# Ranks of two edge tiles from one ScalarE sum, and one set of node rows for both feature halves, in the first layer of a graph network

## The chip, the cores and the metric

The kernel runs on one core of a Trainium2 chip: TensorE (PE in the profile, with its weight loads as PEld), VectorE (DVE), ScalarE (ACT), GpSimd (POOL) and the DMA queues, of which SyncE's (SP) carries most direct transfers. The metric is the device time of one execution in microseconds (us), as the median of repeated executions. Lower is better.

## The reference, cut to what matters

Two graph layers with residual connections and layer norms, on 12,500 nodes with 256 features and 200,000 edges sorted by `dst`.

```python
# first layer: row = src, col = dst
feat = relu(einsum('nd,ohdk->ohnk', x, W) + b)        # o = 2 halves (self, neighbour), 4 heads of 32
feat_self, feat_nei = feat
att_s = leaky(feat_self . a_self); att_n = leaky(feat_nei . a_neigh)
edge_w = (att_s[:, row] + att_n[:, col]) * adj_vals
agg = segment_sum(edge_w * feat_nei[:, col], row)     # sum over the edges of each src node
# both halves: centred and scaled per head, put side by side, then
x = layernorm(x + first_layer)
# second layer: messages relu([x[src], x[dst]] @ W_msg + b), summed by dst, update, layernorm
```

The edges come sorted by `dst`, but the first layer sums by `src`. So the kernel sorts the messages by block of `src`.

## The kernel before, in words

**Three stages run one after the other.** The first builds a log: for each group of 14 tiles of 128 edges (1,792 edges, 112 groups), it makes the messages and scatters them into a DRAM table (`log`), sorted by the block of 128 nodes that their `src` lies in (98 blocks). The second stage reads the log block by block, sums it with matmuls, and finishes the first layer. The third does the second layer with gathers. The change lies in the first stage, and in the loads that the second makes of what the first wrote.

**One group in the first stage, its sort half** (`sort_tasks`). `widen` (L564, ACT) copies the block numbers of the first 7 tiles out to 7 x 99 columns; `hot` (L568, DVE) compares them with a table to make one-hot rows `A`; `hot_b` (L572, DVE) does the other 7 tiles straight from the block numbers with a broadcast operand. `pair` (L576) adds tile t and tile t+7. `ranks`, `quarter`, `rows`, `begins` count and place on PE, ACT and DVE; `keep_v` (L606, ACT) brings the place table `V` (128 x 100) to SBUF. `place_mm` (L622, L624, PE) puts `V` plus 4096 times the one-hot rows into PSUM, in chunks of 5, 5 and 4 tiles, in two buffers `wp`. `place_pick` (L651, ACT) then reads one tile at a time: a relu with bias -4096 leaves the one wanted entry of each row, and `accum_out` sums the row. Each pick is two records in the profile: ACTIVATE and ACTIVATION_READ_ACCUMULATOR. There are 14 picks a group. `split` (L658, L659, L660, DVE) turns the 14 ranks into a partition `q` and a slot `r`; `hot_r` (L664), `hot_q` (L674) and `goods` (L669, DVE) turn them into one-hot operands, and `permute` (L681, PE) carries the edges' data to their places. `extras` (L697, L698, DVE) puts source and weight into the message tile `m`. Destinations go through DRAM (`rel_out` L701, `rel_in` L705, on SP's queue) and come back as a wide row for `hot_n` (L709, DVE). `message` (L718, PE) and `evict` (L725, ACT) make the messages, and four `scatter`s (L731, POOL) write them. `index` (L644, DVE) computes the row indices that the scatters use.

**Its feature half** (`feat_tasks`). A group needs neighbour features of a window of 128 rows that starts at a register's value, `xw`. The self features are made 128 rows at a time in block order, from rows of their own, `xb`, in groups 0 to 97 (98 blocks). Both are loaded on SP's queue (`load_group`, L432, L438), transposed on PE (L457, L460), kept by ACT (`keep`, L466), projected by four 128-column matmuls and a bias matmul (L471, L474), and go through `relu` (L482, ACT) and, on DVE, `att_mult` (L486), `mean_sum` (L491), `att_sum` (L495), `centre` (L500), `leaky_n` (L506) and `leaky_s` (L525). In groups 98 to 111 there are no `xb` rows, and these instructions are half as wide. `out_f` (L528, SP) writes the centred self half to the DRAM table `selfd`; its attention terms stay in SBUF, in `atts`.

**What sets the order.** PE, ACT, DVE and SP execute in the order in which the program emits them. That order is a table: `AT[name]` is a task's place, a group is 256 places after the one before (`TG`), and all tasks of all groups are sorted by `256 * group + AT[name]` and emitted. So a task named 100 of group 3 follows one named 300 of group 2. The numbers set the order alone; an engine starts each instruction as soon as the earlier ones on it and the semaphores allow. Every eighth group also has the `m_` tasks, which prepare the edge data of the next eight groups.

**The second stage** loads `x` and `selfd` per span of up to four blocks (`load_y`), multiplies the summed log by `atts` (`heads_a`, L986) and scales the self half (`own_s`, `own_c`, `own_d`).

Of the kernel before, what the change touches and what calls it, by code (L numbers as in the profile page):

```python
# [11 lines left out]
def _warn_once_fixed(msg, *args, **kwargs):  # L12
# [28 lines left out]
    "widen": -453, "hot": -365, "hot_b": -265, "pair": -179, "ranks": -86, "quarter": -64, "rows": -29,  # L41
    "begins": 13, "keep_begins": 55, "keep_v": 51, "shift": 161, "reach": 262, "steps": 227, "steps_keep": 243,
    "steps_low": 256, "target": 313, "index": 400, "place_mm0": 52, "place_mm1": 63, "place_mm2": 204,
    "pick0": 73, "pick1": 78, "pick2": 78, "pick3": 87, "pick4": 123, "pick5": 144, "pick6": 156, "pick7": 170,
    "pick8": 179, "pick9": 219, "pick10": 229, "pick11": 239, "pick12": 249, "pick13": 280, "split": 339,
    "hot_r": 358, "goods": 374, "hot_q": 371, "permute": 424, "rel_keep": 435, "extras": 477, "rel_turn": 502,
    "rel_row": 552, "rel_out": 574, "rel_in": 595, "hot_n": 959, "message0": 997, "evict0": 1053,
    "message1": 1032, "evict1": 1063, "message2": 1056, "evict2": 1082, "message3": 1065, "evict3": 1121,
    "message4": 1101, "evict4": 1165, "message5": 1188, "evict5": 1203, "scatter0": 1120, "scatter1": 1146,
    "scatter2": 1197, "scatter3": 1206, "load": -331, "transposes": 47, "keep": 68, "project": 80, "relu": 295,  # L50
    "att_mult": 355, "mean_sum": 459, "att_sum": 438, "centre": 467, "leaky_n": 498, "part0": 584, "part1": 636,
    "part2": 665, "part3": 705, "leaky_s": 585, "out_f": 634, "m_load": -1689, "m_cast0": -1234,
    "m_cast1": -1433, "m_col0": -1201, "m_keep0": -1125, "m_col1": -698, "m_keep1": -614, "m_col2": -941,
    "m_keep2": -861, "m_block": -1073, "m_place": -877, "m_high": -378, "m_rest": -285, "m_mid": 263,
    "m_low": 351, "m_win": -76, "m_turn": -866, "m_pairs": -710, "m_mask": -535, "m_count": 210,
}
BIG = 4096.0
# [43 lines left out]
def kernel(  # L101
# [45 lines left out]
    selfd = dram.tile([ROWS, HD], FT, name="selfd")  # L147
# [12 lines left out]
    atts = consts.tile([P, NB, H], FT, name="atts")  # L160
# [55 lines left out]
    with ExitStack() as l0:  # L216
# [28 lines left out]
        nc.vector.memset(nbig, -BIG)  # L245
        quart = dcp.tile([P, 1], FT, name="quart")
# [178 lines left out]
        xb = {}  # L425
        F3 = {}

        def load_group(g):
            if g < NG:
                b = base_reg(g) if g else 0  # L430
                xw[g] = xin.tile([P, D], FT, name="xw")
                nc.sync.dma_start(xw[g], x[bass.ds(b, P), :])  # L432
            if g < NB:
                xb[g] = xin.tile([P, D], FT, name="xb")
                n = min(P, N - g * P)
                if n < P:
                    nc.vector.memset(xb[g], 0.0)
                nc.sync.dma_start(xb[g][:n], x[g * P:g * P + n, :])  # L438

        def feat_tasks(g):  # L440

            ww, bb = g < NG, g < NB
            o0, o1 = (0 if bb else 1), (2 if ww else 1)
            lo, hi = o0 * HD, o1 * HD
            st = {}

            def flat(t):
                return t[:, lo:hi]

            def heads(t):  # L450
                return t[:, lo:hi].rearrange("p (a k) -> p a k", k=32)

            def transposes():
                tp = ps.tile([P, 512], FT, name="tp", bufs=1)
                if ww:
                    for c in range(2):
                        nc.tensor.transpose(tp[:, c * P:(c + 1) * P], xw[g][:, c * P:(c + 1) * P], ident)  # L457
                if bb:
                    for c in range(2):
                        nc.tensor.transpose(tp[:, (2 + c) * P:(3 + c) * P], xb[g][:, c * P:(c + 1) * P], ident)  # L460
                st["tp"] = tp

            def keep():
                xT = feat.tile([P, 4, P], FT, name="xT")
                a, z = (0 if ww else 2), (4 if bb else 2)
                nc.scalar.copy(xT[:, a:z].rearrange("p c q -> p (c q)"), st["tp"][:, a * P:z * P])  # L466
                st["xT"] = xT

            def project():
                fp = bank[g][:, 0:D] if ww else ps.tile([P, 512], FT, name="fs")[:, 0:D]  # L470
                nc.tensor.matmul(fp[:, lo:hi], ones3, bias3[:, lo:hi], start=True, stop=False)  # L471
                for o in range(o0, o1):
                    for c in range(2):
                        nc.tensor.matmul(  # L474
                            fp[:, o * HD:(o + 1) * HD], st["xT"][:, (2 + c) if o == 0 else c, :],
                            w0s[:, c, o * 4:(o + 1) * 4, :].rearrange("p a k -> p (a k)"),
                            start=False, stop=(o == o1 - 1 and c == 1))
                st["fp"] = fp

            def relu():  # L480
                st["R"] = feat.tile([P, D], FT, name="R")
                nc.scalar.activation(flat(st["R"]), st["fp"][:, lo:hi], AF.Relu)  # L482

            def att_mult():
                st["tm"] = feat.tile([P, D], FT, name="tm")
                nc.vector.tensor_tensor(flat(st["tm"]), flat(st["R"]),  # L486
                                        atb.rearrange("p o h k -> p (o h k)")[:, lo:hi], op=OP.mult)

            def mean_sum():
                st["m"] = feat.tile([P, 2 * H], FT, name="m")  # L490
                nc.vector.tensor_reduce(st["m"][:, o0 * H:o1 * H], heads(st["R"]), AX.X, OP.add)  # L491

            def att_sum():
                st["a"] = feat.tile([P, 2 * H], FT, name="a")
                nc.vector.tensor_reduce(st["a"][:, o0 * H:o1 * H], heads(st["tm"]), AX.X, OP.add)  # L495

            def centre():
                st["F"] = feat.tile([P, D + H], FT, name="F", bufs=4)
                m = st["m"][:, o0 * H:o1 * H]
                nc.vector.scalar_tensor_tensor(  # L500
                    heads(st["F"]), m[:, :, None].to_broadcast([P, (o1 - o0) * H, 32]), -1.0 / 32, heads(st["R"]),
                    op0=OP.mult, op1=OP.add)

            def leaky_n():
                a = st["a"][:, H:2 * H]
                nc.vector.scalar_tensor_tensor(st["F"][:, D:D + H], a, 0.2, a, op0=OP.mult, op1=OP.max)  # L506


            def part(k):
                def f():  # L510
                    n = st["F"][:, HD:]
# [11 lines left out]
            def leaky_s():  # L523
                a = st["a"][:, 0:H]
                nc.vector.scalar_tensor_tensor(atts[:, g, :], a, 0.2, a, op0=OP.mult, op1=OP.max)  # L525

            def out_f():
                nc.sync.dma_start(selfd[g * P:(g + 1) * P, :], st["F"][:, 0:HD])  # L528

            w = lambda f: f if ww else None  # L530
            k = lambda f: f if bb else None
            return dict(transposes=transposes, keep=keep, project=project, relu=relu,
                        att_mult=att_mult, mean_sum=mean_sum, att_sum=att_sum, centre=centre, leaky_n=w(leaky_n),
                        part0=w(part(0)), part1=w(part(1)), part2=w(part(2)), part3=w(part(3)),
                        leaky_s=k(leaky_s), out_f=k(out_f))
# [12 lines left out]
        def sort_tasks(g):  # L548
# [5 lines left out]
            CH = [(0, 5), (5, 5), (10, 4)]  # L554
# [7 lines left out]
            def widen():  # L562
                st["bx"] = srt.tile([P, h, NBX], BF, name="bx")
                nc.scalar.copy(st["bx"], blk[c][:, j * GT:j * GT + h, None].to_broadcast([P, h, NBX]))  # L564

            def hot():
                st["A"] = srt.tile([P, GT, NBX], BF, name="A", bufs=3)
                nc.vector.tensor_tensor(st["A"][:, :h], iotab[:, :h], st["bx"], op=OP.is_equal)  # L568

            def hot_b():  # L570
                b = blk[c][:, j * GT + h:j * GT + GT, None].to_broadcast([P, h, NBX])
                nc.vector.tensor_tensor(st["A"][:, h:], iotab[:, h:], b, op=OP.is_equal)  # L572
# [32 lines left out]
            def keep_v():  # L605
                nc.scalar.copy(small("v", NBE, FR, p=P), st["V"])  # L606
# [10 lines left out]
            def place_mm(i):  # L617
                def f():
# [3 lines left out]
                    nc.tensor.matmul(o, identr, st["v"][:, None, :].to_broadcast([P, n, NBE]),  # L622
# [23 lines left out]
            def place_pick(t):  # L646
                def f():
                    i, k = divmod(t, 5)
                    if t == 0:
                        small("sl", GT, p=P)  # L650
                    nc.scalar.activation(small("junk", NBX, BF, p=P), st["w", i][:, k * NBE:k * NBE + NBX], AF.Relu,  # L651
                                         bias=nbig, accum_out=st["sl"][:, t:t + 1])
                return f

            def split():
# [1035 lines left out]
```

## Time and profile before

| What | Value |
|---|---|
| median of 10 runs | 4409.63 us (4402.7 to 4414.29) |
| the profiled execution | 4414.53 us, its span 4412.8 us |
| busy over the span | PE 3698.7, PEld 3132.3, DVE 3159.6, ACT 2372.6, POOL 2660.0 us |
| first stage | the first `hot_q` (L674) starts at 29.4 us, the last at 1052.9 us, the last message matmul (L718) at 1075.3 us |
| second stage | its log matmuls (L972) from 1087.9 to 1998.1 us |
| L651, the picks | 1,568 ACTIVATE, 604.8 us busy, and 1,568 accumulator reads, 477.4 us busy |

A row of groups reads: line, engine, operation, output <- inputs, shapes, count, then busy time and the mean ns of one instruction, then the idle time of the engine just before them and what ended it. A mean is the length of the record. Records of one engine overlap, so what an instruction costs its engine when it is full is the distance from its start to the next start, which the timeline shows. A windows row gives, for a stretch of the span, the busy time of each engine with its instruction count, the granted TensorE clock, and the DMA share.

### The profile page before, as it was taken

To read this page: it belongs to the slowest core of one execution; us is meant where nothing else is said; L and a number is where in the kernel's file an instruction comes from. 1 tells how busy PE (TensorE), PEld (TensorE's weight loads), DVE (VectorE), ACT (ScalarE), POOL (GpSimd) and SP (SyncE) were. 2 spreads that over 40 slices of the span, in tenths; PEclk is the share of its full clock that TensorE was granted. 3 is DMA by queue.
4 is the path that set the end of the run, shared out by engine and by line. 5 is a ranking of instruction groups with operands and counts; after the bars stand their busy time and mean duration, and the time that the engine had idled before them with its cause. 6 is when DMAs were issued, how large, how long until landed. Compare 5 with 4: busy or idle time off the path is not lost. (4 is left out here: it accounts for less than half of the span.)

```text
span 4412.8 us, 82564 instructions
## 1 busy us (share of the span) xinstructions
PE 3698.7 (84%) x24976; PEld 3132.3 (71%) x24976; DVE 3159.6 (72%) x9205; ACT 2372.6 (54%) x8379; POOL 2660.0 (60%) x2542
## 2 busy tenths in 40 slices
PE   8999999997999999996777777777777777777776
PEld 6888888876888888885666666666566666656665
DVE  9999999997999999995555555555555555555555
ACT  7999999996222222224444444444444444444444
POOL 2545555555666666665666666666666666666664
PEclk9999999998999999998888888888898888888888
DMA  5877766666666666664555555555555555545553
GB/s 187 277 266 273 247 216 216 218 202 215 181 192 191 191 191 191 191 183 132 143 143 143 141 141 146 140 142 144 141 143 143 143 143 142 146 138 143 143 143 109
DMA packets 470159, 763.55 MB, mean 173 GB/s; under 512 B 76202, under 2 KB 313504, under 8 KB 469712
## 3 DMA queue, kind: packets, MB, share of 16 engines
q1 hardware_dynamic: 339552, 415.13, 33.0%
q0 software_dynamic: 110848, 327.87, 24.3%
q10 hardware_dynamic: 19312, 15.21, 1.1%
q8 instruction: 204, 3.34, 0.3%
q14 instruction: 243, 1.99, 0.2%
HBM read 559.81 MB, written 198.12 MB: 172 GB/s over the span
## 5 line engine op out<-in xcount | busy, mean ns | idle before, releaser
L1346 POOL DMA_INDIRECT gb<-pd,srcf x1563 | 1501.0, 960 | 889.0 <-issue 492.5
L1424 PE MATMUL agg<-gb,o 128*128 128x256 f32 x3126 | 941.6, 429 | 346.9 <-ACT gb L1407 234.1
L1405 DVE TENSOR_TENSOR gb<-qp,gb 128x512 f32<-128x512 f32 x781 | 531.4, 680 | 757.0 <-remote 368.3
L1424 PEld LDWEIGHTS agg<-gb,o 128*128 128x128 f32 x3126 | 647.6, 215 | 520.4 <-ACT gb L1407 282.9
L731 POOL DMA_INDIRECT log<-m,ix x448 | 545.6, 1218 | 531.7 <-ACT rT L693 195.5
L1407 ACT ACTIVATE gb<-gb 128x512 f32<-128x512 f32 x781 | 487.4, 627 | 675.8 <-DVE gb L1405 483.9
L972 PE MATMUL sum<-lg,o 128*128 128x256 f32 x3724 | 838.3, 379 | 12.9 <-DVE o L964 12.8
L972 PEld LDWEIGHTS sum<-lg,o 128*128 128x128 f32 x3724 | 696.0, 189 | 112.5 <-POOL lg L959 12.4
L964 DVE TENSOR_SCALAR o<-iotap,lg 128x128 f32<-128x128 f32 x1862 | 613.2, 397 | 42.9 <-PE sum L972 35.1
L651 ACT ACTIVATE junk<-wp,nbig 128x99 bf16<-128x99 f32 x1568 | 604.8, 461 | 1.4 <-PE wp L624 1.0
L1383 PE MATMUL qp<-qh,oT 128*128 128x256 f32 x1563 | 595.4, 400 | 2.8 <-issue 1.9
L959 POOL TENSOR_TENSOR lg<-lg 128x512 f32<-128x512 f32 x392 | 429.6, 1108 | 229.6 <-DMA lg<-log 169.9
L651 ACT ACTIVATION_READ_ACCUMULATOR junk<-wp,nbig 128x1 f32 x1568 | 477.4, 318 | 0.0
L1383 PE MATMUL qp<-ql,oT 128*128 128x256 f32 x1563 | 438.1, 300 | 0.3 <-issue 0.3
L718 PE MATMUL mp<-F,oT 128*128 128x132 bf16 x5376 | 419.3, 222 | 20.0 <-ACT m L725 8.3
L718 PEld LDWEIGHTS <-oT 128*128 128x128 bf16 x5376 | 344.0, 99 | 52.3 <-issue 18.9
L1391 ACT ACTIVATE o<-iotac,rel 128x128 f32<-128x128 f32 x782 | 267.9, 391 | 177.5 <-PE agg L1424 49.8
L725 ACT COPY m<-mp 128x396 f32<-128x396 f32 (+1 forms) x672 | 352.3, 569 | 15.1 <-PE mp L718 10.0
L1383 PEld LDWEIGHTS qp<-qh,oT 128*128 128x128 f32 x1563 | 330.6, 212 | 29.3 <-PE agg L1424 2.3
L1383 PEld LDWEIGHTS qp<-ql,oT 128*128 128x128 f32 x1563 | 329.3, 211 | 24.8
L1387 DVE TENSOR_TENSOR o<-iotac,rel 128x256 f32<-128x256 f32 x390 | 161.5, 414 | 247.4 <-PE agg L1424 68.0
L890 PE MATMUL qm<-wms,xT 128*128 128x256 f32 x224 | 96.7, 521 | 254.4 <-ACT xT L885 211.6
(263 smaller groups left out, 6561.8 us busy)
## 6 DMA issues: line engine op xcount, KB each, us to landing
lg<-log SPq DMA_DIRECT2D x392, 268.0 KB
dr<-in_dst_dram SPq DMA_DIRECT2D x781, 128.0 KB
rr<-reld SPq DMA_DIRECT2D x112, 512.0 KB
log<-zero SPq DMA_DIRECT2D x101, 268.0 KB
gb<-pd,srcf POOLq DMA_INDIRECT x1563
lg<-log SPq DMA_DIRECT2D x98, 201.0 KB
xw<-in_x_dram SPq DMA_DIRECT2D x112, 128.0 KB
xw<-x1d SPq DMA_DIRECT2D x112, 128.0 KB
```

Source lines behind the costliest of these rows:

```text
L651: nc.scalar.activation(small("junk", NBX, BF, p=P), st["w", i][:, k * NBE:k * NBE + NBX], AF.Relu, bias=nbig, accum_out=st["sl"][:, t:t + 1])
L718: nc.tensor.matmul(mp[:, r * (HD + H):(r + 1) * (HD + H)], st["oT"][:, r0 + r], F3[g][:, k], start=(k == 0), stop=(k == 2))
L725: nc.scalar.copy(st["m"][:, r0:r0 + n, 0:HD + H], st.pop(("mp", i))[:, :n * (HD + H)].rearrange("p (r w) -> p r w", r=n))
L731: ins = nc.gpsimd.indirect_dma_start(out=log[:, :], out_offset=bass.IndirectOffsetOnAxis(ap=st["ix"][:, k:k + 1], axis=0), in_=st["m"][:, ...
L959: e.tensor_tensor(t[:, 1, :n, 0:HD].rearrange("p r (h k) -> p r h k", h=H), t[:, 0, :n, 0:HD].rearrange("p r (h k) -> p r h k", h=H), t[:, ...
L964: nc.vector.tensor_scalar(o[:, r], iotap, t[:, 0, r, MW - 2:MW - 1], t[:, 0, r, MW - 1:MW], op0=OP.is_equal, op1=OP.mult)
L972: nc.tensor.matmul(sums[b], o[:, r], t[:, :, r, 0:HD], start=(k == 0 and r == 0), stop=(k == NK - 1 and r == n - 1))
L1346: nc.gpsimd.indirect_dma_start(out=gb[s][:r, i], out_offset=None, in_=pd[:, :], in_offset=bass.IndirectOffsetOnAxis(ap=srci[:r, t:t + 1], ...
L1383: nc.tensor.matmul(qp[:r, i], oT[:, i * P:i * P + r], q, start=(k == 0), stop=(k == 1))
L1405: nc.vector.tensor_tensor(z, qp, z, op=OP.add)
L1407: nc.scalar.activation(z, z, AF.Relu)
L1424: nc.tensor.matmul(agg[g], o[:r, i], z[:r, i], start=(j == 0 and i == 0), stop=lastmm)
```

## The change: packed picks, a full widen, one set of rows, and a new order

Six edits and a new table of places:

1. The place table is kept twice, once as it is and once times 2048 (`keep_w`, a new ACT instruction). `place_mm` adds the plain one to even tiles and the other to odd tiles, in chunks of 4, 4, 4 and 2 tiles; the one-hot factor is 2^23 in place of 4096. One `place_pick` now reads two tiles (2 x 99 columns) and sums both into one number, even rank plus 2048 times odd rank: 7 picks a group.
2. The numbers are taken apart again by `unpack` (one ACT instruction on 128 x 7) and two more DVE instructions on 128 x 7 at the head of `split`.
3. `widen` copies all 14 tiles, and `hot_b` reads the copy as `hot` does.
4. The self half is projected from the window rows `xw` too. The `xb` rows, their loads, transposes and copies go; two matmuls of 256 columns take the place of four of 128. All 112 groups now make both halves, and `out_f` writes 132 columns (self half and its attention terms) to a window of `selfd` that starts at the register's value. Windows overlap, and write the same values where they do.
5. `atts` goes; the second stage loads 132 columns per row, and `heads_a` reads the attention terms there (the tile `fs` has three buffers for two).
6. The copy of the source column into `m` leaves `extras` (DVE) and becomes `src_keep` (ACT).

```diff
 AT = {
-    "widen": -453, "hot": -365, "hot_b": -265, "pair": -179, "ranks": -86, "quarter": -64, "rows": -29,
...
-    "pick8": 179, "pick9": 219, "pick10": 229, "pick11": 239, "pick12": 249, "pick13": 280, "split": 339,
...
+    "widen": -324, "hot": -281, "hot_b": -274, "pair": -190, "ranks": -115, "quarter": -70, "rows": -56,
+    "begins": -10, "keep_begins": 37, "keep_v": 33, "shift": 133, "reach": 236, "steps": 165, "steps_keep": 227,
+    "steps_low": 283, "target": 292, "index": 365, "keep_w": 37, "place_mm0": 64, "place_mm1": 77,
+    "place_mm2": 216, "place_mm3": 244, "pick0": 103, "pick1": 108, "pick2": 164, "pick3": 179, "pick4": 247,
+    "pick5": 247, "pick6": 250, "unpack": 267, "split": 308, "hot_r": 370, "goods": 402, "hot_q": 360,
+    "permute": 453, "rel_keep": 457, "extras": 491, "src_keep": 520, "rel_turn": 513, "rel_row": 535,
...
-BIG = 4096.0
+BIG = 2.0 ** 23
+PACK = 2048.0
...
         def load_group(g):
...
-            if g < NB:
-                xb[g] = xin.tile([P, D], FT, name="xb")
...
+            xreg[g] = base_reg(g) if g else 0
+            xw[g] = xin.tile([P, D], FT, name="xw")
+            nc.sync.dma_start(xw[g], x[bass.ds(xreg[g], P), :])
...
             def project():
...
+                nc.tensor.matmul(fp, ones3, bias3, start=True, stop=False)
+                for c in range(2):
+                    nc.tensor.matmul(fp, st["xT"][:, c, :], w0s[:, c].rearrange("p a k -> p (a k)"),
+                                     start=False, stop=(c == 1))
...
+            def leaky_s():
+                a = st["a"][:, 0:H]
+                nc.vector.scalar_tensor_tensor(st["F"][:, 0:H], a, 0.2, a, op0=OP.mult, op1=OP.max)
...
             def out_f():
-                nc.sync.dma_start(selfd[g * P:(g + 1) * P, :], st["F"][:, 0:HD])
+                nc.sync.dma_start(selfd[bass.ds(xreg[g], P), :], st["F"][:, 0:H + HD])
...
-            CH = [(0, 5), (5, 5), (10, 4)]
+            CH = [(a, min(4, GT - a)) for a in range(0, GT, 4)]
...
             def widen():
-                st["bx"] = srt.tile([P, h, NBX], BF, name="bx")
-                nc.scalar.copy(st["bx"], blk[c][:, j * GT:j * GT + h, None].to_broadcast([P, h, NBX]))
+                st["bx"] = srt.tile([P, GT, NBX], BF, name="bx")
+                nc.scalar.copy(st["bx"], blk[c][:, tl, None].to_broadcast([P, GT, NBX]))
...
             def hot_b():
-                b = blk[c][:, j * GT + h:j * GT + GT, None].to_broadcast([P, h, NBX])
-                nc.vector.tensor_tensor(st["A"][:, h:], iotab[:, h:], b, op=OP.is_equal)
+                nc.vector.tensor_tensor(st["A"][:, h:], iotab[:, h:], st["bx"][:, h:], op=OP.is_equal)
...
+            def keep_w():
+                nc.scalar.activation(st["v"][:, NBE:], st["V"], AF.Copy, scale=PACK)
...
-            def place_pick(t):
+            def place_pick(k):
                 def f():
-                    i, k = divmod(t, 5)
...
-                    nc.scalar.activation(small("junk", NBX, BF, p=P), st["w", i][:, k * NBE:k * NBE + NBX], AF.Relu,
-                                         bias=nbig, accum_out=st["sl"][:, t:t + 1])
+                    i, t = k // 2, 2 * k % 4
...
+                    nc.scalar.activation(
+                        small("junk", 2 * NBX, BF, p=P).rearrange("p (t b) -> p t b", b=NBX),
+                        st["w", i][:, t * NBE:(t + 2) * NBE].rearrange("p (t b) -> p t b", b=NBE)[:, :, :NBX],
+                        AF.Relu, bias=nbig, accum_out=st["s7"][:, k:k + 1])
...
+            def unpack():
+                nc.scalar.activation(small("t7", h, p=P), st["s7"], AF.Identity, bias=nhalf, scale=1.0 / PACK)
+
             def split():
-                sl = st["sl"]
+                sl = small("sl", GT, p=P)
+                odd = sl.rearrange("p (k w) -> p k w", w=2)[:, :, 1]
+                nc.vector.tensor_scalar(odd, st["t7"], MAGIC, -MAGIC, op0=OP.add, op1=OP.add)
+                nc.vector.scalar_tensor_tensor(sl.rearrange("p (k w) -> p k w", w=2)[:, :, 0], odd, -PACK, st["s7"],
+                                               op0=OP.mult, op1=OP.add)
...
             def extras():
                 m = st["m"] = msgp.tile([P, NR, MW], FT, name="m")
-                nc.vector.tensor_copy(m[:, :, MW - 2], st["go"][:, :, 1])
                 nc.vector.tensor_reduce(m[:, :, MW - 1], st["go"][:, :, 2:5], AX.X, OP.add)
+
+            def src_keep():
+                nc.scalar.copy(st["m"][:, :, MW - 2], st["go"][:, :, 1])
...
-                                    atts[:, b:b + n, :, None].to_broadcast([P, n, H, 32]), op=OP.mult)
+                                    fs.pop(q)[:, :n, 0:H, None].to_broadcast([P, n, H, 32]), op=OP.mult)
```

## The prediction on record

> **What bounds the kernel now.** I read the page's busy slices first, to see which stage the change lies in, then the windows of that stage, then the waits of each engine in it, and last the groups by shape and the timeline of one group.
>
> ```profile
> DVE  9999999997999999995555555555555555555555
> ACT  7999999996222222224444444444444444444444
> ```
>
> One slice is 110 us. In the first nine (the stage that builds the log) ACT and DVE are both full. From the tenth, ACT falls to 2: the second stage isn't ACT's. So an edit that relieves ACT can pay in the first stage alone, and there only if DVE lets it. The windows (us, then busy time and count per engine, clock, DMA share) show the same:
>
> ```profile
> 200.00:400.00 200.00, 190.56 (x2345) 161.28 (x2344) 193.54 (x605) 196.03 (x979) 101.33 (x85) 1.00 0.79 269
> 400.00:620.00 220.00, 211.65 (x2611) 179.41 (x2609) 213.49 (x666) 216.26 (x1072) 116.95 (x95) 1.00 0.71 241
> 620.00:920.00 300.00, 291.32 (x3611) 247.59 (x3610) 294.87 (x930) 299.53 (x1493) 164.00 (x132) 1.00 0.66 217
> 990.00:1050.00 60.00, 56.90 (x728) 48.16 (x728) 55.75 (x180) 60.00 (x317) 30.15 (x28) 1.00 0.61 200
> ```
>
> From 620 to 920 us ACT is busy 299.5 of 300 us, DVE 294.9, PE 291.3 (columns: PE, PEld, DVE, ACT, POOL). In this stretch the answer on DVE's waits is empty, and so is ACT's. DVE's missing 5 us are gaps of 0.03 us between an instruction and one that reads its result. So **DVE has no spare time either**: two engines are full at once, at 9.16 us a group (`hot_q` starts at 626.8 us and, 24 groups on, at 846.7). In 200 to 1000 us DVE waited on others for 6 us in all:
>
> ```profile
> DVE ix L644 <- DMA log<-m,ix: 2.2, 2, 1.5
> DVE ix L644 <- PE mp L718: 1.1, 1, 1.1
> ```
>
> **The change part by part.** A full engine's price is the distance from start to start, so I take prices from one group's timeline and use the shape rows to see that they repeat.
>
> *ACT.* Picks start at 700.35, 700.68 and 701.00: 0.325 us each, 14 make 4.55. A copy costs 0.48 for 512 columns (699.67 to 700.15) and 0.15 for 132 (703.87 to 704.02), so 0.87 ns a column; 99 more columns add 0.09. Seven picks of 198: 7 x 0.415 = 2.9, saving 1.65. `xT` of 256 columns costs 0.27 (as `relu`, 706.98 to 707.25) for 0.48: -0.21 in 98 groups. Added: 693 columns of `widen` +0.60, `keep_w` +0.13 (as `keep_v`, 707.40 to 707.53), `unpack` +0.14 (as `quarter`, 704.41 to 704.55), `src_keep` +0.06 (as `rel_keep`, 704.02 to 704.08). Sum: -0.93 us a group; in the last 14, where `relu` doubles (+0.10) and `xT` saves nothing, -0.62. Over the stage: 98 x 0.93 + 14 x 0.62 = 100 us less ACT work. That is the size of the edit, not its worth, since DVE stays.
>
> *DVE.* These lines are the price list (line, shape, count, then busy us and mean ns; below, the timeline: start, length):
>
> ```profile
> L572 DVE TENSOR_TENSOR A<-iotab,blk 128x693 bf16<-128x693 bf16 x33 | 28.8, 873 | 0.0
> ...
> L568 DVE TENSOR_TENSOR A<-iotab,bx 128x693 bf16<-128x693 bf16 x32 | 16.4, 511 | 0.0
> ```
>
> ```profile
> 713.17 0.41 DVE L491 TENSOR_REDUCE m<-R 128x8 f32<-128x256 f32 x1
> 713.61 0.43 DVE L500 SCALAR_TENSOR_TENSOR F<-m,R 128x256 f32<-128x256 f32 x1
> 713.96 0.18 DVE L697 COPY m<-mp 128x16 f32<-128x16 f32 x1
> 714.04 0.20 DVE L698 TENSOR_REDUCE m<-mp 128x16 f32<-128x48 f32 x1
> ...
> 716.18 0.17 DVE L658 SCALAR_TENSOR_TENSOR sl<-sl,twin 128x14 f32<-128x14 f32 x1
> 716.38 0.18 DVE L659 TENSOR_SCALAR q<-sl 128x14 bf16<-128x14 f32 x1
> 716.60 0.17 DVE L660 TENSOR_TENSOR r<-sl,q 128x14 bf16<-128x14 f32 x1
> 716.69 0.42 DVE L486 TENSOR_TENSOR tm<-R,atb 128x256 f32<-128x256 f32 x1
> ```
>
> - `hot_b` takes the form of `hot`: 873 to 511 ns, -0.36.
> - The copy L697 leaves: 713.96 to 714.04, -0.08.
> - `centre` (L500) reads what L491 wrote just before it, and starts 0.44 after it; the same reduce L495, with an unrelated successor, is followed after 0.33 (711.97 to 712.30). In the new order `mean_sum` and `centre` are apart: -0.11.
> - `split` grows from three dependent instructions to five. Each that the next one waits for costs 0.20 to 0.22 (L658, L659); the last costs 0.09. Two more: +0.42.
>
> Sum: **-0.13 us a group**. DVE's relief from `hot_b` is nearly eaten by the unpacking. The dependent pair is not in the trace on 7 columns; between 14 and 7 nothing should change, as the time is start-up. Bounds: from 0.08 each (an independent small one, L697) to 0.22, so the sum lies between -0.39 and -0.11. I take 0.21, the row of the same chain.
>
> In the last 14 groups DVE also gains width: L486, L491, L495 and L500 were 298, 278, 278 and 296 ns and become 430, 410, 410 and 424 (+0.52), and `leaky_s` adds 0.07. There ACT is the full engine (60.0 of 60) and DVE has 55.75, which is 8.09 us of each 8.7 us group. With +0.59 - 0.13 DVE reaches 8.55, and its gaps of 0.15 make 8.7. So those groups stay where they are: 0.
>
> [...]
>
> *PE.* The two `xb` transposes go (-0.14, 607.14 to 607.28); four projections of 128 columns become two of 256, the same columns; the `place_mm` columns are the same in one more pair, whose fixed part I put at 0.09 from the 500- and 400-column pairs (0.54 and 0.45 start to start). Net -0.05, off the path as long as DVE is fuller.
>
> *SP and DMA.* 98 loads of 128 KB go. `out_f` issues 14 more and waits for the write before it, a group ago: nothing, as SP has nine microseconds for five issues. `rel_in` and `load` are named later, but SP waits only for `rT` and for the `rel_out` landing, so in fact it issues them early in the slot. In the second stage PE is 200 of 200 us busy (1200 to 1800 us): wider `fs` rows cost nothing there. *POOL*: four scatters a group as before, half busy.
>
> *Fill and drain*: 29 us before the first `hot_q` and 22 us after the last are chains of latency through the same engines; I leave them, within 2 us.
>
> Sum: 98 x -0.13 = -13, last 14 groups 0, on the profiled execution's 4414.5 us (span 4412.8 and 1.7 around it): 4401.5. The median of the runs is 4.9 below that execution, so **4396.5 us**, -0.3%.
>
> **The rivals.**
>
> *A. ACT was the limit and all its relief shows:* 4409.6 - 100 = 4310. For it: ACT's 299.5 of 300. Against: DVE's waits are empty over 300 us; an engine that never waits cannot be sped up by another.
>
> *B. PE takes over.* PE's 291.3 of 300 is 8.90 us a group, DVE's new need 9.03. Light groups (8.62 us, without `m_` tasks) would ask 8.5 of DVE, below PE's average, and PE cannot catch up fully in the heavy ones (10.2 us) with two buffers. If half the groups give nothing, 49 x 0.13 = 6 us remain: 4403, within what a run can tell. Against: matmul records are pipelined, and PE's weight loads, which run beside them, fill 247.6 of 300. PE also has 4.7 us of waits on `rows` there, so it isn't full.
>
> *C. Slower: DVE waits in `split`.* The first new instruction reads `unpack`, which stands on ACT behind three picks in a row (1.25 us), `src_keep` and `relu` (0.33), all behind `permute` and two `place_mm` on PE. Behind `goods`, DVE has some 3.8 us of other work until `split`; the chain over PE (0.95) and ACT (0.06 + 0.04 + 0.27 + 1.25 + 0.06 + 0.14) needs 2.8, and a little for hand-overs. So 0.9 us of slack, if PE is on time. If PE comes late by more, DVE stands still, every group, and everything queued behind `split` with it (`pair`, `hot_q`, `index`, `goods`, on which PE's `permute` waits). Each 0.1 us is 11 us; the gain is gone from 0.13 us a group on, and at 0.3 us: 4409.6 + 112 x 0.17 = 4429.
>
> *D. `hot_b` stays at its old price* though it reads `bx` (its half starts 693 columns in, at an odd element). Then -0.36 falls away: +0.23 x 112 = 4435. Against: `pair` (L576) reads that same odd half of `A` in 515 ns; an output at an odd element beside dense inputs is in no row. [...]
>
> **How the numbers follow.** Forecast 0.52, A 0.03, B 0.22, C 0.19, D 0.04. The forecast's own range runs from the cheap end of the pair (98 x 0.39 = 38: 4371) to the dear one (4399). The range takes most of it, B and C's middle, and leaves out A, D and C's tail: 4375 to 4426. A difference of 0.2% (8.8 us) is about what runs of this kernel tell from none. Faster than that: 0.53. Within: 0.25, B and some ends of its neighbours. Slower: 0.22, C and D.
>
> **What would show it.** In 620 to 920 us of the changed kernel: DVE near 295 with no waits and 24 groups in 217 us; ACT down to about 270 with idle time; `hot_b`'s row at about 511 ns; starts of the new pair 0.2 us apart. If DVE's waits name `unpack` it is C; if they name PE's matmuls, B. I am wrong if the small instructions cost much less than 0.2 us, or if `index`, whose place moves from 218 to 166 places behind the scatter that frees its buffer, begins to wait for that landing in many groups: its 2.2 us of waits would grow.

## The result: slower, 4444.32 us

| | before | after |
|---|---|---|
| median of the runs | 4408.15 us (4402.7 to 4414.29, 28 runs) | 4444.32 us (4433.74 to 4449.16, 8 runs) |
| ratio | | 1.008, 95% interval 1.0071 to 1.0088 |
| profiled execution, span | 4414.53, 4412.8 us | 4434.49, 4432.7 us |
| last message matmul of the first stage starts at | 1075.4 us | 1102.5 us |
| log matmuls of the second stage, first to last | 911 us | 911 us |

The change costs 36 us, where a gain of 13 was forecast. In the two profiled executions the first stage is 27 us longer, the second is the same, and the third came out 7 us shorter; so in this pair the loss lies in the first stage. The profiled execution of the changed kernel is at the low end of its runs, which spread over 15 us, so the pair differs by 20 us where the medians differ by 36; what makes the runs spread is not settled.

The busy slices of the changed kernel: in the first nine, neither ACT nor DVE is full any more.

```profile
DVE  8999999997899999995555555555555555555555
ACT  7898989997122222223444444444444444444444
```

The windows of the first stage (us, then busy time and count of PE, PEld, DVE, ACT, POOL, clock, DMA share):

```profile
200.00:400.00 200.00, 186.90 (x2194) 158.15 (x2190) 186.50 (x604) 177.15 (x716) 115.50 (x84) 0.98 0.73 245
400.00:620.00 220.00, 206.25 (x2478) 175.56 (x2479) 208.46 (x681) 198.82 (x809) 127.76 (x93) 1.00 0.68 227
620.00:920.00 300.00, 283.35 (x3389) 241.29 (x3387) 286.06 (x934) 273.85 (x1102) 178.68 (x127) 0.99 0.59 198
990.00:1050.00 60.00, 56.39 (x673) 47.88 (x672) 57.13 (x189) 53.95 (x218) 38.17 (x27) 1.00 0.61 198
```

From 620 to 920 us PE, DVE and ACT are all less busy (291.3 to 283.4, 294.9 to 286.1, 299.5 to 273.9); POOL alone is busier (164.0 to 178.7), and still idle for two fifths of the time. When the engines that were full no longer are, and the stage is longer, they wait for each other. The largest of DVE's waits, 200 to 1000 us (who, for whom, us in all, times, longest):

```profile
DVE rows L565 <- ACT rows L561: 8.9, 23, 1.9
DVE ix L622 <- DMA log<-m,ix: 3.4, 6, 1.1
DVE mi L362 <- ACT srcf L352: 1.9, 6, 0.4
DVE ix L622 <- issue: 1.8, 4, 0.8
DVE ix L622 <- PE mp L707: 1.4, 2, 1.2
DVE rows L565 <- issue: 0.9, 4, 0.3
DVE ix L622 <- PE wp L602: 0.9, 2, 0.5
```

There are two places: `rows` (DVE) stands for `quarter` (ACT), and `index` for the landing of the scatters whose buffer it takes. The names in the second are not to be trusted singly: the waits of that one line, 9.0 us in all, bear six names in the view. The same view for PE:

```profile
PE mp L707 <- ACT m L687: 18.0, 41, 1.2
PE mp L668 <- DVE mv L656: 6.1, 23, 0.4
PE fs L569 <- DVE rows L565: 5.5, 7, 0.8
```

PE's largest wait is for `src_keep` (L687), the copy moved to ACT. The DVE instructions themselves are as forecast. The first two lines are groups by shape (busy us, mean ns), the rest is the timeline of one group:

```profile
L543 DVE TENSOR_TENSOR A<-iotab,bx 128x693 bf16<-128x693 bf16 x32 | 16.5, 517 | 0.2
L546 DVE TENSOR_TENSOR A<-iotab,bx 128x693 bf16<-128x693 bf16 x32 | 16.4, 512 | 0.0
```

```profile
715.55 0.16 DVE L641 TENSOR_SCALAR sl<-t 128x7 f32<-128x7 f32 x1
715.75 0.17 DVE L642 SCALAR_TENSOR_TENSOR sl<-sl,s 128x7 f32<-128x7 f32 x1
715.95 0.18 DVE L645 SCALAR_TENSOR_TENSOR sl<-sl,twin 128x14 f32<-128x14 f32 x1
```

`hot_b` fell from 873 to 512 ns, and the new pair starts 0.20 us apart.

### The profile page after: what moved, and what is told of

The parts are those of the page before. It is cut to its first block, busy times and chain, and to the rows that moved or that the text cites. A ratio compares the mean times of both kernels' runs of the same rounds, so it can differ in the third digit from the quotient of the medians.

```text
span 4432.7 us, 81040 instructions
## 1 busy us (share of the span) xinstructions
PE 3697.6 (83%) x24612; PEld 3129.1 (71%) x24612; DVE 3162.6 (71%) x9332; ACT 2309.8 (52%) x7147; POOL 2738.0 (62%) x2542
## 5 line engine op out<-in xcount | busy, mean ns | idle before, releaser
L720 POOL DMA_INDIRECT log<-m,ix x448 | 620.4, 1385 | 483.8 <-ACT v L583 304.5
L962 PE MATMUL sum<-lg,o 128*128 128x256 f32 x3724 | 838.6, 379 | 12.4 <-POOL lg L949 11.4
L629 ACT ACTIVATE junk<-wp,nbig 128x198 bf16<-128x198 f32 x784 | 331.0, 439 | 28.5 <-PE fs L558 18.7
L714 ACT COPY m<-mp 128x396 f32<-128x396 f32 (+1 forms) x672 | 295.8, 442 | 68.7 <-PE fs L558 35.0
L1367 DVE TENSOR_SCALAR oT<-dr,baseP 128x256 fp32r<-128x256 int32 x782 | 282.2, 361 | 11.2 <-DMA dr<-in_dst_dram 11.2
```

Source lines behind the costliest of these rows:

```text
L629: nc.scalar.activation(small("junk", 2 * NBX, BF, p=P).rearrange("p (t b) -> p t b", b=NBX), st["w", i][:, t * NBE:(t + 2) * NBE].rearrang ...
L714: nc.scalar.copy(st["m"][:, r0:r0 + n, 0:HD + H], st.pop(("mp", i))[:, :n * (HD + H)].rearrange("p (r w) -> p r w", r=n))
L720: ins = nc.gpsimd.indirect_dma_start(out=log[:, :], out_offset=bass.IndirectOffsetOnAxis(ap=st["ix"][:, k:k + 1], axis=0), in_=st["m"][:, ...
L962: nc.tensor.matmul(sums[b], o[:, r], t[:, :, r, 0:HD], start=(k == 0 and r == 0), stop=(k == NK - 1 and r == n - 1))
```

## The experiments

Each kernel was measured against the kernel before on its own chip, and the chips differ in the clock of the third stage. These are two windows of g2 (the kernel before with six `ix` buffers), one in the first stage and one in the third:

```profile
200.00:400.00 200.00, 194.34 (x2402) 165.00 (x2402) 196.43 (x619) 199.70 (x995) 104.06 (x87) 1.00 0.80 274
2100.00:3000.00 900.00, 735.10 (x3796) 592.37 (x3795) 581.25 (x1610) 508.72 (x1241) 683.96 (x710) 0.99 0.62 171
```

The granted clock (third column from the end) is 0.99 in that third stage, and was 0.87 there on the chip of the first profiles. The kernel before took 4374 and 4378 us beside e1 to f4 and 4007 to 4009 beside the others, in place of 4408. In the first stage, where the change acts, its clock is 1.00 on both chips. The changed kernel had 0.98 to 1.00 there, but so has h3 below, which is faster than before (0.99 from 620 to 920 us in both), so this clock doesn't explain the loss. Below I compare **microseconds over before** (the difference of the medians on the same chip), next to the ratio.

| kernel | over before, us | ratio, 95% interval |
|---|---|---|
| the change | +36.2 | 1.008 (1.0071 to 1.0088) |
| e1: copy on DVE again | +27.1 | 1.0058 (1.0041 to 1.0075) |
| e2: `src_keep` early | +33.0 | 1.0076 (1.0059 to 1.0093) |
| e3: before's order | +19.8 | 1.0043 (1.0027 to 1.006) |
| e3b: before's order, copy on DVE | +17.8 | 1.0037 (1.0022 to 1.0051) |
| f1: `quarter` early | +27.1 | 1.0074 (1.0047 to 1.0102) |
| f2: six `ix` buffers | +6.5 | 1.0018 (1.0007 to 1.0028) |
| f3: f1 and f2 | +8.3 | 1.0017 (1.0008 to 1.0027) |
| f4: f3 and e2 | +20.0 | 1.005 (1.0033 to 1.0068) |
| g1: before, `index` early | +120.1 | 1.0306 (1.0277 to 1.0334) |
| g2: before, six `ix` buffers | -3.9 | 0.9989 (0.9979 to 0.9999) |
| g3: e3b without two TENSOR_SCALARs | +1.7 | 1.0004 (0.9994 to 1.0014) |
| g4: many pairs apart | +77.4 | 1.0196 (1.0179 to 1.0213) |
| h1: g3, copy on ACT, six buffers | -5.2 | 0.9988 (0.9978 to 0.9997) |
| h2: h1, rounding on ACT | +11.9 | 1.0029 (1.0018 to 1.0041) |
| h3: six buffers and `rows` later | **-11.7** | 0.9966 (0.9952 to 0.998) |
| h4: h3, `widen` early | -7.7 | 0.9981 (0.9971 to 0.999) |
| i1: `rows` later alone | +9.4 | 1.002 (1.001 to 1.0029) |
| i2: i1, and `index` later | +14.2 | 1.004 (1.0025 to 1.0054) |

### Is it the copy on ACT, or the order? (e1, e2, e3, e3b)

My first theory, R, came from PE's largest wait: `src_keep` holds `permute`'s PSUM buffer too long. Its rivals were O (the order) and W (the new operations cost more than thought).

```diff
 # e1: in extras, and src_keep gone
+                nc.vector.tensor_copy(m[:, :, MW - 2], st["go"][:, :, 1])
 # e2
-    "src_keep": 520
+    "src_keep": 458
 # e3, e3b: before's places for all steps that both kernels have (e3b with the edit of e1)
-    "widen": -324, "hot": -281, ... "quarter": -70, "rows": -56, ... "index": 365
+    "widen": -453, "hot": -365, ... "quarter": -64, "rows": -29, ... "index": 400
```

> The changed kernel with one edit taken back: the copy of the sources is in extras on DVE again, and the ACT step src_keep is gone. Theory R (ring): src_keep stands behind rel_keep, dh, relu and three picks on ACT and holds the permute result's PSUM buffer, so that PE's message waits 18.0 us for it between 200 and 1000 us; ACT's picks and evictions are then late, and DVE's rows and index wait. R expects that PE wait to be gone, DVE's waits at rows and index to fall from about 18 us to under 8, and the time to fall from 4444 to 4410 to 4428, net of about 9 us of copies (112 times 0.085 us) that DVE takes back. Theory O (order): the order of the table as a whole, with quarter and rows 14 places apart and the index earlier, makes DVE's waits; it expects the PE wait to go but the time to stay within 6 us of 4444 or to rise by the 9 us. Theory W (work): the packed chain itself (picks, unpack, the pair in split) is dearer than it looked; it expects 4440 to 4455.

> The changed kernel with src_keep left on ACT but moved from place 520 to 458, just behind rel_keep, so that it is ahead of relu and the picks of the next group. R expects PE's wait for it gone or under 3 us, and 4405 to 4425, below the kernel with the copy on DVE by up to 9 us. O expects 4438 to 4448. W expects 4438 to 4448.

> All of the change's operations, in the order of before: every step that both kernels have is at before's place, and the new ones lie beside their old neighbours (keep_w 52, place_mm3 216, picks 78 87 123 156 219 239 249, unpack 280, src_keep 478). R expects a part of the loss to stay, as src_keep is still behind rel_keep and picks on ACT: 4405 to 4430. O expects the forecast of the change to come true: 4385 to 4405. W expects 4430 to 4450, as the operations are the same.

> The same as the kernel in before's order, and the copy of the sources in extras on DVE. DVE then has the changed kernel's work plus 0.085 us a group, 0.04 us a group less than before. R expects 4398 to 4412, the lowest or near the lowest of the four; O expects 4390 to 4412, 5 to 10 us above the one in before's order with the copy on ACT; W expects 4435 to 4455.

**R fell.** In both e1 and e2 PE's wait for the copy is gone, but PE stands instead at a step that needs ACT, where it stood 1.1 us in the changed kernel (e1 first, then e2):

```profile
PE tp L429 <- ACT rT L664: 14.7, 31, 0.9
```

```profile
PE tp L429 <- ACT rT L664: 20.7, 42, 1.3
```

The time falls by 9 and 3 us, the second within the intervals. Taking away the longest wait of an engine with idle time only moved it. Before's order took away nearly half of the loss, so order matters, but the 4385 to 4405 us that O expected (on a before of 4409: 4 to 24 us under it) did not come. W missed its ranges too, in three of the four, by 2 to 9 us; g3 below shows what was true of it.

### The two waits of DVE (f1 to f4)

Theory T was that the new order has set `quarter` and `rows` too near to each other, 14 places for 35.

```diff
 # f1
-    "quarter": -70
+    "quarter": -91
 # f2
-  small("ix", RW, I32, bufs=4, p=P)
+  small("ix", RW, I32, bufs=6, p=P)
 # f3: both.  f4: both, and e2
```

> The changed kernel with one step moved: quarter goes from place -70 to -91, so that it stands 35 places ahead of rows, as in the kernel before, and not 14. Theory T (tight pairs): DVE's wait at rows is there because the new order leaves 14 places between the two steps; T expects that wait to fall from 11 us between 200 and 1000 us to under 4, the index wait to stay, and a ratio to before of 1.002 to 1.006. Theory R (PE is late because of src_keep, and everything behind it): the wait only moves to another step, ratio 1.006 to 1.010.

> The changed kernel with six buffers in place of four for the tile ix, so that index no longer waits until the scatters of four groups before have landed. Nothing is moved. T expects the wait of index for the log's transfers (3.4 us, with some 5 us put down to other things) to be gone, the wait at rows to stay, ratio 1.004 to 1.008. If the names in the view of waits are right and only the 3.4 us are due to the transfers, the ratio stays at 1.007 to 1.009. R expects 1.006 to 1.010.

> Both of these edits: quarter at -91 and six buffers for ix. T expects DVE's waits beyond the 0.17 us a group between dependent small steps to fall under 0.1 us, groups of 9.0 to 9.2 us between 620 and 920, and a ratio of 0.992 to 1.001, at or below before. R expects 1.004 to 1.010, with PE's wait for src_keep still 10 us or more.

> Both edits, and src_keep at place 458 on ACT, just behind rel_keep. T and R together expect the least time of all: ratio 0.988 to 0.999. If PE becomes the limit at its 8.8 to 8.9 us a group, the ratio is 0.992 to 0.996. If it stays over 1.002, there is a third cause that neither names.

**Six buffers for `ix` take away 30 of the 36 us**, though nothing is moved and only 3.4 us of waits carried the transfers' name. DVE's waits in f2, 200 to 1000 us:

```profile
DVE rows L565 <- ACT rows L561: 5.0, 10, 0.9
DVE rows L565 <- ACT junk L629: 1.8, 3, 0.6
DVE mi L362 <- ACT srcf L352: 0.9, 4, 0.2
DVE F L497 <- ACT F L495: 0.7, 2, 0.5
DVE ix L622 <- PE wp L602: 0.5, 1, 0.5
```

The waits of `index` fell from about 9 us in all to 0.5. From the end of the fourth scatter on POOL to the start of the `index` four groups on, the trace of before has 5.5 us in the median and 3.2 at the least; after has 4.2 and 1.9. That is theory L: **landing**. Moving `quarter` earlier cured `rows` (0.4 us left in f1) and passed the wait on to `hot`, since ACT then stands at `quarter` (14 us, for 3 in the changed kernel), ahead of `widen`:

```profile
DVE A L527 <- ACT bx L523: 7.5, 22, 0.6
```

So f3 is no better than f2, and with `src_keep` early (f4) it is worse: PE's wait at `tp` for `rT` is 30.8 us there. f1, f2 and f3 came out outside T's ranges, f2 far below its own: T had one of two causes. By its own expectation f4's 1.005 asks for a third; beyond this wait none was found.

### Landing from the other side, the held step, and a failed repair (g1 to g4)

In e3b DVE has hardly a wait (0.9 us in 800), and yet a group takes 9.38 us, by the starts of `hot_q`. The timeline shows where the time is:

```profile
654.27 0.98 POOL L702 DMA_INDIRECT log<-m,ix  x1 [1.71 <-ACT m L696]
...
654.83 0.40 DVE L625 TENSOR_SCALAR sl<-t 128x7 f32<-128x7 f32 x1
655.25 0.17 DVE L626 SCALAR_TENSOR_TENSOR sl<-sl,s 128x7 f32<-128x7 f32 x1
```

L625 is the first new step of `split`. It takes 0.17 us in the median of 85 groups, and 0.40 here: it begins with 0.42 us of a scatter left on POOL, and ends 0.03 us before the scatter does. All six long ones between 600 and 760 us lie so. I called this H, held by POOL.

```diff
 # g1, on the kernel before
-    "index": 400
+    "index": 348
 # g2, on the kernel before: bufs=6 for ix
 # g3, on e3b (less1 and less2 are constant tiles)
-  nc.vector.tensor_scalar(odd, st["t7"], MAGIC, -MAGIC, op0=OP.add, op1=OP.add)
+  nc.vector.scalar_tensor_tensor(odd, st["t7"], MAGIC, less1[:, :h], op0=OP.add, op1=OP.add)
-  nc.vector.tensor_scalar(q, sl, MAGIC * NR, -MAGIC * NR, op0=OP.add, op1=OP.add)
+  nc.vector.scalar_tensor_tensor(q, sl, MAGIC * NR, less2, op0=OP.add, op1=OP.add)
 # g4, on the change: bufs=6 for ix, src_keep 458, and
-    "rows": -56, "begins": -10, "transposes": 54, "keep": 71
+    "rows": -40, "begins": 4, "transposes": 80, "keep": 98
```

> The kernel before with one step moved: index goes from place 400 to 348, so that it stands 166 places behind the last scatter of four groups earlier, whose buffer it takes, as in the changed kernel, and not 218. Theory L (landing): the changed kernel loses because index, and behind it ranks on PE, waits until those scatters have landed; L expects DVE's wait at index to grow from 4 us between 200 and 1000 us to 8 or more and the time to rise by 10 to 28 us (ratio 1.002 to 1.0065). Theory T (only the tight pair quarter and rows, or the operations themselves) expects no change, ratio 0.9985 to 1.0015.

> The kernel before with six buffers for ix in place of four: the control. L expects a gain of no more than the 4 us that DVE stands at index: ratio 0.998 to 1.000. If it gains as much as the changed kernel did from this edit (0.6%), the buffers are simply a better size for any order, and L says nothing of the change.

> All of the change's operations in before's order, the copy of the sources in extras on DVE, and two of the steps in split (the one that rounds the odd ranks, and the one that makes q) written as SCALAR_TENSOR_TENSOR with a constant tile in place of TENSOR_SCALAR. Theory H (held by POOL): these two TENSOR_SCALARs took up to 0.40 us and not 0.17 when they began in the last 0.5 us of a scatter's time on POOL, while the SCALAR_TENSOR_TENSORs beside them never did; H expects no such long ones, some 0.14 us a group less on DVE and a ratio of 1.000 to 1.002, where the same kernel with TENSOR_SCALAR had 1.0037. If any small DVE step is held there, the ratio stays at 1.003 to 1.005.

> The changed kernel with every pair that was seen waiting set farther apart: six buffers for ix, rows at -40 and begins at 4, src_keep at 458, transposes at 80 and keep at 98. L and T together expect DVE's waits beyond the dependent small steps to fall under 0.1 us a group and a ratio of 0.990 to 1.000, the least of all kernels here. If PE's lateness is passed on to another step, 1.001 to 1.004.

**g3 confirms H.** The groups of e3b and of g3, 620 to 920 us (busy us, mean ns):

```profile
L625 DVE TENSOR_SCALAR sl<-t 128x7 f32<-128x7 f32 x32 | 8.0, 250 | 0.0
L630 DVE TENSOR_SCALAR q<-sl 128x14 bf16<-128x14 f32 x32 | 7.8, 245 | 1.1
```

```profile
L629 DVE SCALAR_TENSOR_TENSOR sl<-t,less 128x7 f32<-128x7 f32 x32 | 5.1, 160 | 0.0
L634 DVE SCALAR_TENSOR_TENSOR q<-sl,less 128x14 bf16<-128x14 f32 x32 | 5.6, 174 | 1.1
```

In the other form the same steps have means of 160 and 174 ns, for 250 and 245, and are never long in g3's trace. A group falls from 9.38 to 9.22 us, and the loss from 17.8 to 1.7. **g2** says that six buffers are worth only 4 us to the kernel before, which waited 4 us at `index`: the cure belongs to the changed order. **g1 doesn't tell**: the time rose by 120 us, but the view does not name the scatters:

```profile
DVE ix L628 <- ACT xT L450: 50.7, 44, 2.9
DVE ix L628 <- PE fs L624: 20.6, 22, 4.0
```

In groups 23 to 102 `index` waits 73 times, and 71 times it starts 0.09 to 0.10 us after the last matmul of `target`, its own input. So the run has nothing to say on the landing; it shows what one step moved by 52 places can cost. **g4 was a bad repair**: `transposes` at 80 falls behind a chunk of `place_mm` on PE, and ACT stands before the next picks.

```profile
ACT xT L433 <- PE tp L429: 85.9, 72, 2.2
```

### What is left, and a version that beats both (h1 to h4, i1, i2)

```diff
 # h1, on g3: src_keep on ACT at 436, bufs=6 for ix
 # h2, on h1: t7 plus MAGIC, then minus MAGIC, by two ACTIVATEs into sl; the first step of split gone
 # h3, on f2
-    "rows": -56, "begins": -10
+    "rows": -40, "begins": 4
 # h4, on h3: widen -400 for -324
 # i1: h3's places, with four buffers for ix
 # i2, on i1: index 392 for 365, ranks -104 for -115
```

> All of the change's operations in before's order, src_keep on ACT at place 436 just behind rel_keep, six buffers for ix, and split's two rounding steps as SCALAR_TENSOR_TENSOR. Every cause named so far is taken away: the landing of the scatters, the step held by POOL, the copy in the middle of ACT's queue. By DVE's own steps a group is then 0.08 us shorter than with the copy on DVE (9.21 us), so 9.10 to 9.15; the forecast of the change (0.13 us a group less than before) expects a ratio of 0.997 to 0.999. If a wait for dh or for the picks comes instead, 1.000 to 1.004.

> The same, and the rounding of the odd ranks on ACT in two ACTIVATEs that add and take away 1.5 times 2 to the 23, in place of one step of split on DVE. DVE loses 0.20 us a group, ACT gains 0.42 us in a stage in which it has 0.9 us idle. If DVE is the limit, groups of 8.9 to 9.0 us and a ratio of 0.993 to 0.997; if split then stands for unpack, 0.997 to 1.003.

> The changed kernel with six buffers for ix, and rows at -40 and begins at 4. With the buffers alone it had a ratio of 1.0018 and DVE stood 7 us at rows between 200 and 1000 us. If these 7 us are the rest of the loss, the ratio is 1.0005 to 1.0015. If the tight pair is a sign of a late PE and no cause, 1.0015 to 1.004.

> The one before, and widen at -400 in place of -324, so that it no longer stands on ACT behind quarter. If hot's wait for widen and ACT's queue at that place are part of the rest, the ratio falls by another 0.0005 to 0.002; if not, it stays within 0.0005, or rises if evictions now stand behind widen.

> The changed kernel with rows at -40 and begins at 4, and four buffers for ix as in the change. With six buffers these two places took the kernel from 6.5 us over before to 11.7 us under it. If the pair quarter and rows is a cause of its own, this kernel is some 15 to 20 us under the changed one: 14 to 24 us over before, ratio 1.0035 to 1.006, with the wait at index still there. If the pair only matters once the index is free, 30 to 38 us over, 1.0075 to 1.0095. If the pair was the whole cause, 5 us over or less.

> The changed kernel with index moved from place 365 to 392 and ranks from -115 to -104, four buffers for ix. The index is then 193 places behind the scatter whose buffer it takes, and not 166 (218 before). It sets the landing of the scatters apart from what else more buffers could do (where tiles lie): L expects the index wait to shrink and a ratio of 1.002 to 1.005; if the buffers helped in another way, 1.007 to 1.010. If ranks, 22 places behind the index of two groups earlier, then stands on PE for it, L could be masked and the ratio stays over 1.006 with a wait of ranks for index in the view.

**h3 is the fastest kernel of the study**, 11.7 us under before. The whole answer on its DVE waits, 200 to 1000 us:

```profile
DVE F L481 <- ACT F L479: 1.5, 5, 0.5
DVE oT L682 <- DMA rr<-reld: 0.8, 1, 0.8
DVE A L527 <- ACT bx L523: 0.6, 2, 0.4
DVE ix L606 <- PE fs L602: 0.5, 2, 0.3
```

Its window, and the start of `hot_q` 24 groups apart:

```profile
620.00:920.00 300.00, 284.97 (x3521) 247.07 (x3519) 291.82 (x970) 283.77 (x1145) 187.45 (x133) 0.99 0.60 205
```

```profile
620.00 1.08 DVE L645 TENSOR_TENSOR qh<-iotaq,q 128x1792 bf16<-128x1792 bf16 x1
...
837.30 1.08 DVE L645 TENSOR_TENSOR qh<-iotaq,q 128x1792 bf16<-128x1792 bf16 x1
```

24 groups in 217.3 us, 9.05 a group, and `src_keep` at its place of the change: PE's wait for it is no longer in the answer. PE now waits for DVE (36.3 us for `hot_n`'s result), the engine that sets the pace. With i1 the table of the two causes is full:

| over before, us | `rows` at -56, `begins` at -10 | `rows` at -40, `begins` at 4 |
|---|---|---|
| four `ix` buffers | +36.2 | +9.4 |
| six | +6.5 | -11.7 |

Either cure takes away 27 to 30 us, the second another 18 to 21. With 4 to 6 us of uncertainty on each cell, it is clear that each counts by itself; that it counts for more in company is not. i1 falls between the ranges that had been given for it (14 to 24 us, and 5 or less). It moves `rows` and `begins` together, and takes PE's wait for `src_keep` away as h3 does; the two moves were not tried apart. In i1 the wait at `index` is left, and now bears its name:

```profile
DVE ix L606 <- DMA log<-m,ix: 8.9, 13, 2.4
```

i2 was to tell the landing from a gain through where tiles lie, and doesn't. Its expectation takes it for the changed kernel with `index` moved, but it has `rows` at -40 and `begins` at 4 as well: its neighbour is i1 (+9.4), and not the change (+36.2). With `index` 27 places later the waits that bear the landing's name fall from 8.9 to 0.9 us, but the time doesn't fall (+14.2), as DVE's `part1` now stands 11.4 us for ACT's `part0`.

The kept traces tell more. This is one of i1's waits: the fourth scatter of four groups before, the last matmul of `target`, and `index`:

```profile
494.23 0.98 POOL L704 DMA_INDIRECT log<-m,ix  x1 [0.30 <-DVE rows L549]
...
496.67 0.16 PE L602 MATMUL fs<-dw,Z 99*128 99x1 bf16 x1
...
500.01 0.16 DVE L606 TENSOR_TENSOR ix<-fs,roww 128x4 int32<-128x4 f32 x1 [1.75 <-DMA log<-m,ix]
```

The input is there at 496.8 us, and `index` starts 3.2 us later. In groups 23 to 102 `index` waits 16 times in the changed kernel and 17 times in i1; in 15 and 17 of them it starts more than 1.4 us after `target`. Its other input is a constant, so what it still lacks is its buffer. How long a scatter takes to land, only the trace of g2 shows, for 56 of them (from the start of the record):

```profile
DMA to landing us min/median/max: 2.8/3.6/5.4
```

From the end of the record that is 1.8 to 4.4 us, and `index` comes 4.2 us after the end of the scatter that frees its buffer in the changed kernel, but 22 in f2 (medians). And six buffers make no DVE step shorter: over groups 23 to 102 the lengths of DVE's records add up to 10.87 us a group in the changed kernel and 10.88 in f2, while its idle time falls from 0.50 to 0.34. So the buffers helped through waits, and not through faster steps.

h1 has the change's operations in before's order with nothing left to hide their gain: 9.17 us a group. But six buffers alone are worth 3.9 us to the kernel before (g2). Of h1's 5.2 us that leaves 1.3 to the change, less than the intervals tell from none, and of h3's 11.7 it leaves 7.8. h2 takes 0.20 us more from DVE and loses: `att_mult` then stands 11.8 us for `relu`, which is behind the new ACTIVATEs. h4's earlier `widen` gained nothing over h3 (-7.7 and -11.7).

## Why the prediction was wrong, step by step

- **DVE as the limit, with no spare time: right.** The kernels that gained (g2, h1, h3, h4) have 0 to 6.5 us of DVE waits from 200 to 1000 us, the changed kernel 22.6.
- **ACT's relief has no worth of its own: right.** ACT's busy time fell from 9.15 us a group (299.5 of 300, times 9.16) to 8.56 in h3 (283.8 of 300, times 9.05): 0.6, not 0.93 (in the changed kernel `src_keep` takes 0.20 us from start to start and `unpack` 0.21, medians from 620 to 920 us, where 0.06 and 0.14 were put down). The group fell by 0.11, which is near DVE's sum and far from ACT's, so the mis-sized terms cost nothing.
- **DVE's prices, sum -0.13 us a group: right.** `hot_b` 512 ns for 511, the pair 0.20 apart for 0.21. h3 gives the 24 groups in 217 us that the forecast asked for; g2, the kernel before with the same six buffers, needs 220.6, which is 0.14 a group more. In the whole time h3 gains 7.8 us over g2 where the sum said 13.
- **The step that failed is "98 x -0.13"**: it multiplies DVE's work by the groups as if DVE went on without waits in the new order. Two moves of the order were given no price. One was seen: `index`, 166 in place of 218 places behind the scatter that frees its buffer, stood in the last sentence as a way to be wrong, but in no term, no rival and not in the range. Six buffers, which take this wait away, are worth 21 to 30 us. The other was not seen: `quarter` and `rows`, 35 places apart before and 14 after; setting them farther apart is worth 18 to 27.
- **Rival C had the mechanism and the wrong place.** DVE did stand for an ACT that comes late, but at `rows` and not at `split`: the waits of the changed kernel do not name `unpack`. What makes ACT late at `quarter` was not taken apart further; more places in front of `rows` cure it.
- **Rival A, D: refuted** (ACT is busy 273.9 of 300 us in the changed kernel; `hot_b`, with its output at an odd element, runs at 512 ns, no dearer than `pair` with its input there, 515 ns before). **B: not reached.** PE is at 285 of 300 us in h3.
- **The last 14 groups at 0: nearly.** From the 99th `hot_q` to the last, before needs 114.6 us, the changed kernel 118.5, h3 115.1.

## What to carry to other kernels

When a change brings a new order, list every pair of producer and consumer on different engines, and every reuse of a buffer whose reader is a transfer, with the distance before and after; those that shrink belong in the sum with a price, even when the trace of before shows almost no wait there. The longest wait in the view may be a follower: of two kernels that only removed PE's 18 us, neither gained 10, while a larger ring for a tile of four columns gained 30. Try a spare buffer before a move: f1, f4, g1, g4 and i2 each moved a step, and each made another pair wait. And give the spare buffer to the kernel before as well (g2), or its gain is taken for the change's.

## What the runs showed of the hardware

In e3b two DVE TENSOR_SCALARs, on 7 columns (L625) and on 14 (L630), were long when they began near the end of a scatter on POOL. Those that began with 0.31 to 0.44 us of a scatter left took 0.28 to 0.41 us for 0.16 to 0.18, and ended 0.02 to 0.03 us before it: 30 of 85 groups for the one step, 39 for the other (by more than 0.05 us). Those that began with 0.47 us or more left were not longer. Written as SCALAR_TENSOR_TENSOR the two steps were never long in g3 (87 groups, means of 160 and 174 ns); why the one form is held and the other not, no run shows. The view of waits does not list this (0.9 us of DVE's waits in e3b): it is in the length of the record. In the changed kernel's own order the two steps seldom met the end of a scatter (L641 had a mean of 168 ns), so it is no part of the 36 us.

In g2 the 56 indirect scatters whose landing was traced landed 1.8 to 4.4 us after the end of their record on POOL, so the end of the record does not tell when. `index` waits for the landing: in the wait of i1 shown above it starts 4.8 us after the end of the scatter's record.
